# Attention outputs of six batches by seven products in a two-layer gated cross-attention kernel (one core)

## The chip, the cores and the metric

The kernel runs on one core of a Trainium2 chip. The metric is the device time of one launch in microseconds (us); the time of a version is the median of its runs. The engines are TensorE (PE; its weight loads are shown apart as PEld), VectorE (DVE), ScalarE (ACT), GpSimd (POOL) and SyncE (SP), which starts the DMAs. Each engine works through its own queue in order. Matrix products are written to PSUM, in banks of 512 float32 values for each of 128 partitions; an engine must read a bank out before it is written anew.

## The reference

Everything is float32. `x` is 8 batches of 512 tokens by 512 features; `ctx` is 8 batches of 120 keys by 512 features.

```python
x = x + tanh(g_xattn[0]) * L0_xattn(layernorm(x), ctx)         # 16 heads of 32, no mask
x = x + tanh(g_ffn[0])   * L0_ffn(layernorm(x))                # routed: 32 experts x 4 sets
x = x + tanh(g_xattn[1]) * L1_xattn(layernorm(x), ctx, mask)   # with biases
x = x + tanh(g_ffn[1])   * L1_ffn(layernorm(x))                # channel mix: gate, key, value

# an attention:
q, k, v = heads(y @ Wq.T), heads(ctx @ Wk.T), heads(ctx @ Wv.T)
out = softmax(q @ k.T / sqrt(32)) @ v          # for each head
return merge(out) @ Wo.T
```

The change touches the two attentions: the product with `Wo` above all, and the order of the work around it.

## The kernel before

**Tiles.** The 4096 tokens are 32 tiles of 128, four to a batch. `CrossAttention` is built twice (layer 0 and layer 1) and goes through three parts.

**Load and prologue.** The constructor loads, projects the keys (L342), and calls `prologue`: the values of the batches (`project_values`, L361, four products of 512 columns for a batch; it also has VectorE take the layer-norm sums of batch b+3), the transposes of the normalized tokens of batches 0 and 1 (`transpose_x`, L421, with the copy by ScalarE at L422, and `normalize` on ScalarE at L406, two buffers), the queries of batch 0, and the scores of tile 0. Here the order of every engine's queue is that of the program text (`manual_schedule(engines=every)`).

**Slots.** `run` goes through tiles t. A slot is: the scores of tile t+1 (L489, into the two double banks of `p_s`), products that stand ahead of the transposes, the transposes of the probabilities of tile t (L546, into the same double banks), more products, then `attend` (L581). In `run` only TensorE (and SP in layer 1) keeps the order of the program; the queues of VectorE, ScalarE and GpSimd are put in order by the planner when the program is compiled, from when it takes each instruction to be ready. An instruction that is ready and comes first in the program goes first.

**Softmax of a tile** (`scores`): VectorE reduces a maximum over each half (L514, L525); ScalarE takes eight exponentials of 120 columns with their sums (L517, which free one double bank); VectorE subtracts (L527, which frees the other), ScalarE takes one exponential of 960 columns (L528); VectorE sums (L533); GpSimd scales twice (L507).

**Seven products.** The queries of a batch (512 x 512 x 512) are done by `SevenProducts`: the two matrices are cut in quarters, and seven products of quarter sums take the place of eight. One product is `multiply`: four matmuls of 256 columns, which the profile shows as eight instructions (L149), since a float32 matmul is two. The sums of weights are taken once, those of tokens for each batch (L107).

**Outputs.** `output` takes four matmuls of 512 columns for a tile (L598, eight instructions), and VectorE adds the bank, times the gate, to `x` (L607). `run` splits them: two or three of the four ahead of the transposes, the rest behind.

**Banks.** `p_mm` has four single banks for everything else: query products, outputs, transposed tokens, `attend`.

**Late transposes.** `transpose_probs_late` (L567) takes four single banks of `p_mm` instead of the two of `p_s`, so that it need not wait for the exponentials of the next tile; VectorE copies one of the four (L569), ScalarE three (L571). Before the change only `tail` uses it, for the last five tiles.

**Beside attention.** `after` calls `RoutedFfn.in_slot` in layer 0 (layer-norm, a DMA of the tile to DRAM, transposes L722, routing products L731, three tiles behind) and `ChannelMix.in_slot` in layer 1.

Of the kernel before, what the change touches and what calls it, by code (L numbers as in the profile page):

```python
# [17 lines left out]
P = 128  # L18
# [53 lines left out]
class SevenProducts:  # L72
# [24 lines left out]
    @staticmethod  # L97
    def right_steps(w, t1, t2, t3, t4, engine):

        b11, b12, b21, b22 = [quarter(w, c, h) for c in (0, 1) for h in (0, 1)]

        def step(*args):
            return lambda: engine.tensor_tensor(*args)  # L107

        return [
            step(t3, b22, b12, ALU.subtract),  # L110
            step(t1, b12, b11, ALU.subtract),
            step(t2, b22, t1, ALU.subtract),
            step(t4, t2, b21, ALU.subtract),
        ]
# [91 lines left out]

class CrossAttention:
# [7 lines left out]
    def __init__(  # L215
        self, cm, tc, es, ins, gate, mask=None, biases=None, loads=(), then=None, vpool=None
    ):
        self.cm, self.nc, self.tc, self.gate, self.then = cm, cm.nc, tc, gate, then
        self.masked, self.biased = mask is not None, biases is not None
        nc = cm.nc  # L220

        def pool(name, bufs, **kw):
            pool = tc.tile_pool(name=name, bufs=bufs, reuse_waits="tile", **kw)
            return es.enter_context(pool)

        self.pool = pool("at_w", 1)
        vpool = vpool or self.pool
        self.norm = pool("at_n", 2)
        self.soft = pool("at_soft", 2)
        self.p_mm = pool("at_mm", 4, space=PSUM)  # L230
        self.p_s = pool("at_s", 2, space=PSUM)
        self.wq = self.pool.tile([P, NC, D], FP, name="wq")
        self.wo = self.pool.tile([P, NC, D], FP, name="wo")
        self.kT = self.pool.tile([P, NC, B * LK], FP, name="kT")
        self.v = [vpool.tile([P, 2, D], FP, name=f"v{q}") for q in range(B // 2)]
        self.xn, self.xnT, self.qT, self.probs, self.aT = {}, {}, {}, {}, {}
        self.ops = {}

        def right(name):
            return tc.tile_pool(name=name, bufs=1, side="right", reuse_waits="tile")  # L240

        with right("at_v") as self.vp:
            with right("at_k") as self.kp:
                self.load(ins, list(loads), mask, biases)
                if self.biased:
                    self.scale_biases()
                self.project_keys()
                if self.biased:
                    nc.gpsimd.tensor_scalar(self.gbo, self.gbo, self.gate, None, ALU.mult)
                for t in range(2):  # L250
                    self.normalize(t)
                if self.masked:
                    self.make_mask()
                self.sum_query_weights()
                for b in (1, 2):
                    self.stats_of_batch(b)
            self.work = pool("at_work", 2)
            self.prologue()

    def load(self, ins, loads, mask, biases):  # L260
# [4 lines left out]

        wv = self.soft.tile([P, NC * D], FP, name="wv", tag="pr")
        self.wv = wv.rearrange("p (c f) -> p c f", c=NC)
# [108 lines left out]
    def prologue(self):  # L376

        for b in range(3):
            self.project_values(b)
        for t in range(2 * TB):  # L380
            self.transpose_x(t)
            self.normalize(t + 2)
            if t < TB - 1:
                self.project_values(t + 3)
            elif t < 2 * TB - 1:
                self.queries(0, t + 1 - TB)
        rest = self.scores(0)
        for b in range(B - 2, B):
            self.project_values(b)
        rest()  # L390

# [21 lines left out]
    def transpose_x(self, t):  # L413
        nc = self.nc
        b, i = divmod(t, TB)
        if i == 0:
            self.xnT[b] = self.work.tile([P, NC, S + 1], FP, name="xnT")
# [4 lines left out]
        nc.scalar.copy(self.xnT[b][:, :, i * P : (i + 1) * P], ps)  # L422
        if i == TB - 1:
            self.start_queries(b)
# [9 lines left out]

    def start_queries(self, b):

        xnT = self.xnT[b][:, :, :S]
        own = self.work.tile([P, 2, 256], FP, name="xns", bufs=1)
        sums = [quarter(xnT, 0, 1), quarter(xnT, 0, 0), own, quarter(xnT, 1, 0)]
        engine = self.nc.gpsimd if b > 1 else self.nc.vector  # L440
# [4 lines left out]
        self.xn7 = SevenProducts.right(xnT, *sums)  # L445

    def queries(self, b, f):

        if f == 0:
            self.qT[b] = self.work.tile([P, NC, S], FP, name="qT")  # L450
            self.q7 = SevenProducts(
                self.nc,
                lambda: self.p_mm.tile([P, 2, 256], FP, name="qps", tag="mm"),
                self.wq7,
                self.xn7,
                {(i, j): quarter(self.qT[b], i, j) for i in (0, 1) for j in (0, 1)},
                lambda: quarter(self.xnT[b], 0, 1),
                bias=(self.bqk[:, 0, 0:2], self.bmore) if self.biased else None,
            )
        self.q7.next(2 if f < TB - 1 else 1)  # L460
        if f == 0:
            for step in self.later_sums:
                step()
# [110 lines left out]
    def attend(self, t):  # L574
# [13 lines left out]
        self.aT[t] = self.work.tile([P, NC, P], FP, name="aT")  # L588
        nc.scalar.copy(self.aT[t], aps)  # L589

    def output(self, t, chunks):

        nc, x = self.nc, self.cm.x
        if 0 in chunks:
            self.ops[t] = self.p_mm.tile([P, D], FP, name="ops", tag="mm")
        ops = self.ops[t]
        for c in chunks:
            nc.tensor.matmul(  # L598
                ops,
                self.aT[t][:, c, :],  # L600
                self.wo[:, c, :],
                start=(c == 0),
                stop=(c == NC - 1),
            )
        if NC - 1 in chunks:
            del self.ops[t], self.aT[t]
            nc.vector.scalar_tensor_tensor(  # L607
                x[:, t, :], ops, self.gate, x[:, t, :], ALU.mult, ALU.add
            )
# [6 lines left out]

    def run(self):

        for t in range(-1, NT - TB - 1):
            if t >= 0:  # L620
                if t + 10 < NT:
                    self.normalize(t + 10)
                self.scores(t + 1)()
            self.queries(*divmod(t + TB + 1, TB))
            self.after(t, 0)


            short = t % TB == TB - 2
            ahead = 3 if short else 2
            if t > 0:  # L630
                self.output(t - 1, range(ahead))
            x_ahead = short and not self.masked
            if x_ahead and t + 9 < NT:
                self.transpose_x(t + 9)
            if t >= 0:
                self.transpose_probs(t)
            if t > 0:
                self.output(t - 1, range(ahead, NC))
            if t + 9 < NT and not x_ahead:
                self.transpose_x(t + 9)  # L640
            self.after(t, 1)
            if t >= 0:
                self.attend(t)
            self.after(t, 2)

    def tail(self):

        for t in range(NT - TB - 1, NT + 1):
# [3 lines left out]
            self.output(t - 1, range(NC))  # L652
# [9 lines left out]
class RoutedFfn:  # L662
# [12 lines left out]
    def __init__(self, cm, tc, es, gate, ins):  # L675
# [5 lines left out]
        self.xT, self.perm = {}, {}  # L681

# [72 lines left out]

    def in_slot(self, s, attention, stage):

        last = NT - TB - 1
        if stage == 2 and 0 <= s - 1:
            self.route_stats(s - 1)  # L760
        if (stage == 2 and (0 <= s - 1 < last - 1 or s == NT)) or (stage == 3 and s > last):
            self.route_norm(s - 1 if stage == 2 else s - 2)
        if stage != (0 if s == NT else 1):
            return
        pool = attention.p_mm
        if s == -1:
            self.start()
        if 0 <= s - 4:
            self.route_logits(s - 4, pool.tile([P, D], FP, name="rlps", tag="mm"))
        if 0 <= s - 3:  # L770
            self.route_x(s - 3, pool.tile([P, D], FP, name="rxps", tag="mm"))
        b = (s - 9) // TB
        if (s - 9) % TB == 0 and 0 <= b < B - 2:
            self.route_back(b, pool.tile([P, D], FP, name="pps", tag="mm"))
# [256 lines left out]
class ChannelMix:  # L1031
# [57 lines left out]
    def in_slot(self, s, attention, stage):  # L1089
# [3 lines left out]
        if stage == 2 and 0 <= s - 2 < NT - 2 * TB:  # L1093
            attention.stats(s - 2)
# [17 lines left out]
        i = s - (NT - 10)  # L1112
        if 0 <= i - 1 < TB:
            self.transpose(i - 1)
        if 0 <= i < TB:
            xn = self.at.norm.tile([P, D], FP, name="xn")
            self.normalize(i, xn)
# [35 lines left out]
    def transpose(self, t):  # L1153
# [3 lines left out]
        if i == 0:  # L1157
            self.yT[b] = self.at.work.tile([P, NC, S + 1], FP, name="yT", tag="xnT")
# [30 lines left out]
    def sum_steps(self, b, m, engine=None):  # L1189
        engine = engine or self.nc.vector  # L1190
        at, mix = self.at, self.mix[b, m]
        if m == 1:
            sums = at.work.tile([P, 4 * 2 * 256 + NC], FP, name="xks", tag="xnT")
# [274 lines left out]
```

## Time and profile before

| | |
|---|---|
| median of 3 runs (lowest, highest) | 1437.04 us (1433.01 to 1438.22) |
| the profiled execution | 1433.48 us, of which the span from the first to the last instruction is 1431.7 us |
| ACT, POOL busy | 772.3 us (54%), 643.9 us (45%) |
| mean granted TensorE clock | 0.998 |

| window of the span, us | what runs | TensorE busy, us |
|---|---|---|
| 10 to 42 | keys, layer 0 | 30.70 |
| 42 to 116 | values, prologue, first slots, layer 0 | 71.24 |
| 166 to 215 | slots, layer 0 | 49.00 of 49.00 |
| 410 to 470 | tail, layer 0 | 59.30 |
| 470 to 690 | routed FFN | 204.66 of 220.00 |
| 722 to 800 | values, prologue, first slots, layer 1 | 75.37 |
| 900 to 1065 | slots, layer 1 | 165.00 of 165.00 |
| 1065 to 1135 | tail, layer 1 | 65.85 |
| 1135 to 1432 | channel mix | 287.72 of 297.00 |

Four slots (one batch) take 49.5 us in layer 0 (the same output group starts at 213.93 and 263.47 in the chain that ended last) and 44.4 us in layer 1 (840.78 and 885.14). The page's row for an engine is its busy time; a row for a group of instructions has the busy time of the group and the mean duration of one. Matmuls overlap in the pipe, so the spacing of their starts is what one costs, not its duration.

### The profile page before, as it was taken

To read this page: it belongs to the slowest core of one execution; us is meant where nothing else is said; L and a number is where in the kernel's file an instruction comes from. 1 tells how busy PE (TensorE), PEld (TensorE's weight loads), DVE (VectorE), ACT (ScalarE), POOL (GpSimd) and SP (SyncE) were. 2 spreads that over 40 slices of the span, in tenths; PEclk is the share of its full clock that TensorE was granted. 3 is DMA by queue.
4 is the path that set the end of the run, shared out by engine and by line. 5 is a ranking of instruction groups with operands and counts; after the bars stand their busy time and mean duration, and the time that the engine had idled before them with its cause. 6 is when DMAs were issued, how large, how long until landed. Compare 5 with 4: busy or idle time off the path is not lost.

```text
span 1431.7 us, 32559 instructions
## 1 busy us (share of the span) xinstructions
PE 1384.2 (97%) x13728; PEld 1068.2 (75%) x13728; DVE 1025.1 (72%) x1457; ACT 772.3 (54%) x1874; POOL 643.9 (45%) x576
## 2 busy tenths in 40 slices
PE   7999999999999998999999999999998999999997
PEld 3577777777776787888557777777776788888886
DVE  2666777777777676777576777777778588887786
ACT  1256666666666445444225665666656555445543
POOL 1425545545443001555375665665646333343331
PEclk9999999999999999999999999999999999999999
DMA  9200000000001347433301000000000000000001
GB/s 300 107 9 24 24 23 23 24 23 16 24 31 46 127 135 231 120 105 87 117 0 60 2 1 2 1 2 2 2 30 2 1 30 30 31 30 30 30 16 45
DMA packets 44886, 69.46 MB, mean 49 GB/s; under 512 B 2891, under 2 KB 20811, under 8 KB 44739
## 3 DMA queue, kind: packets, MB, share of 16 engines
q1 hardware_dynamic: 44451, 67.37, 14.6%
q8 instruction: 108, 1.77, 0.5%
q14 instruction: 39, 0.32, 0.1%
q10 hardware_dynamic: 288, 0.00, 0.0%
HBM read 50.59 MB, written 16.78 MB: 47 GB/s over the span
## 4 chain that ended last, share of the span: by engine, by line
PE 72%; DVE 14%; ACT 6%; POOL 4%; issue 3%; DMA 1%; POOLq 0%; DVEq 0%; ACTq 0%
PE ops L598 15%; PE qps L149 13%; PE tps L546 6%; PE cps L149 5%; PE aps L581 5%; PE s L489 4%; PE kps L342 4%; PE rps L992 3%; PE vps L361 3%; PE rlps L731 2%; PE l1ps L907 2%; PE ops L1013 2%; PE xnps L421 2%; PE l2ps L959 2%; PE gps L880 2%
## 5 line engine op out<-in xcount | busy, mean ns | idle before, releaser
L507 POOL TENSOR_TENSOR pr<-pr,rs 128x960 f32<-128x960 f32 x128 | 228.8, 1790 | 251.9 <-DVE rs L506 233.5
L598 PE MATMUL ops<-wo,aT 128*128 128x512 f32 x512 | 239.6, 594 | 0.7 <-ACT aT L589 0.7
L517 ACT ACTIVATE pr<-s,nmx 128x120 f32<-128x120 f32 x512 | 177.4, 372 | 114.0 <-DVE nmx L514 107.8
L598 PEld LDWEIGHTS ops<-wo,aT 128*128 128x128 f32 x512 | 92.1, 190 | 71.9 <-issue 67.0
L1005 POOL TENSOR_TENSOR r<-r,b 128x1024 f32<-128x1024 f32 x31 | 73.5, 2377 | 142.6 <-ACT r L1004 142.6
L149 PE MATMUL qps<-xnT,wq 128*128 128x256 f32 x512 | 119.6, 381 | 0.0
L546 PEld LDWEIGHTS tps<-ident,pr 128*120 128x120 f32 x864 | 96.8, 138 | 29.5 <-issue 26.2
L525 DVE TENSOR_REDUCE mx<-s 128x8 f32<-128x960 f32 x64 | 74.0, 1156 | 56.9 <-PE s L489 56.9
L517 ACT ACTIVATION_READ_ACCUMULATOR pr<-s,nmx 128x1 f32 x512 | 111.3, 217 | 0.0
L546 PE MATMUL tps<-ident,pr 128*120 128x128 f32 x864 | 104.7, 273 | 2.5 <-ACT pr L517 1.4
L149 PEld LDWEIGHTS qps<-xnT,wq 128*128 128x128 f32 x512 | 95.7, 189 | 15.2 <-issue 1.0
L533 DVE TENSOR_REDUCE sm<-pr 128x8 f32<-128x960 f32 x64 | 73.6, 1150 | 22.1 <-ACT pr L528 22.0
L49 DVE BATCH_NORM_STATS2 bnst<-x 128x6 f32<-128x512 f32 x128 | 86.8, 678 | 1.3
L422 ACT COPY xnT<-xnps 128x512 f32<-128x512 f32 x64 | 38.1, 595 | 82.0 <-PE xnps L421 82.0
L514 DVE TENSOR_REDUCE nmx<-s 128x8 f32<-128x960 f32 x64 | 73.5, 1149 | 6.8 <-PE s L489 6.8
L581 PE MATMUL aps<-prT,v 120*32 120x128 f32 x2048 | 73.3, 278 | 4.5 <-ACT prT L571 2.6
L527 DVE TENSOR_TENSOR pr<-s,mx 128x960 f32<-128x960 f32 x64 | 73.6, 1150 | 0.9
L1258 POOL TENSOR_TENSOR x<-x,cv 128x512 f32<-128x512 f32 x28 | 41.4, 1479 | 70.8 <-DVE cv L1255 70.8
L556 ACT COPY prT<-tps 120x1024 f32<-120x1024 f32 x54 | 55.0, 1019 | 32.9 <-PE tps L546 32.9
L489 PE MATMUL s<-kT,qT 32*128 32x120 f32 x2048 | 71.4, 276 | 0.0
L489 PEld LDWEIGHTS s<-kT,qT 32*128 32x128 f32 x2048 | 66.1, 187 | 6.5 <-issue 6.3
L581 PEld LDWEIGHTS aps<-prT,v 120*32 120x32 f32 x2048 | 53.8, 110 | 18.8 <-issue 8.3
(189 smaller groups left out, 3101.1 us busy)
## 6 DMA issues: line engine op xcount, KB each, us to landing
w<-in_w_dram SPq DMA_DIRECT2D x32, 512.0 KB, 4.8
x<-in_x_dram SPq DMA_DIRECT2D x8, 1024.0 KB, 15.4
aside<-x SPq DMA_DIRECT2D x32, 256.0 KB, 2.0
x<-aside SPq DMA_DIRECT2D x8, 1024.0 KB, 9.8
out_dram<-x SPq DMA_DIRECT2D x14, 512.0 KB, 2.8
ctx<-in_ctx_dram SPq DMA_DIRECT2D x4, 960.0 KB, 11.8
wk<-in_wk_dram SPq DMA_DIRECT2D x3, 1024.0 KB, 11.1
wv<-in_wv_dram SPq DMA_DIRECT2D x3, 1024.0 KB, 5.5
```

What stands on the lines that cost most here:

```text
L49: cm.nc.vector.bn_stats(st, cm.x[:, t, :])
L149: self.nc.tensor.matmul(ps[:, m, :], self.a[a][:, k, m * P : (m + 1) * P], self.b[b][:, k, :], start=(k == 0), stop=(k == 1),)
L489: nc.tensor.matmul(s[j // 2][:, j % 2, hc * LK : (hc + 1) * LK], self.qT[b][r : r + 32, hc, toks], self.kT[r : r + 32, hc, keys], start=no ...
L507: nc.gpsimd.tensor_tensor(pr[:, js, :, :], pr[:, js, :, :], rs[:, js, :, :].to_broadcast([P, 2, NC, LK]), ALU.mult,)
L514: nc.vector.tensor_reduce(nmx, sv[1], AX.X, ALU.max, negate=True)
L517: nc.scalar.activation(pr[:, 2 + j, hc, :], sv[1][:, j, hc, :], AF.Exp, bias=nmx[:, j, hc, :], accum_out=sm[:, 2 + j, hc : hc + 1],)
L525: nc.vector.tensor_reduce(mx, sv[0], AX.X, ALU.max)
L527: nc.vector.tensor_tensor(pv, sv[0], mx.to_broadcast([P, 2, NC, LK]), ALU.subtract)
L533: nc.vector.tensor_reduce(sm[:, :2, :], pv, AX.X, ALU.add)
L546: nc.tensor.transpose(ps[:, jj, hc * P : (hc + 1) * P], pr[:, 2 * u + jj, hc, :], self.cm.ident,)
L581: nc.tensor.matmul(aps[32 * j : 32 * j + 32, hc, :], self.v[b // 2][:LK, b % 2, h * HD : (h + 1) * HD], prT[:, j, hc, :], start=True, stop ...
L598: nc.tensor.matmul(ops, self.aT[t][:, c, :], self.wo[:, c, :], start=(c == 0), stop=(c == NC - 1),)
```

## The change

In `run`, the outputs of batches 0 to 5 are no longer made tile by tile. `SevenAdded`, a new kind of `SevenProducts`, makes them for a whole batch and adds each product from PSUM to the places in `x`, times the gate. The tokens of `attend` are kept for a batch in one buffer `aT`. The sums of tokens (`left_steps`) are taken on VectorE after the last `attend` of the batch, the sums of `Wo` once on GpSimd. `SevenAdded` and the query sums borrow quarters of the coming batch's `qT` as room. The outputs of the tiles of batches 6 and 7 are still made singly.

`slots` lists what stands ahead of the transposes and behind them in each slot. A slot whose tile is the last of a batch (t = 3, 7, ..., 23) uses `transpose_probs_late`, with one product and two token transposes ahead of it; the other three slots of a batch have three products ahead and one behind. `xnT` becomes a single buffer. In the prologue only the values of batches 0 to 4 are made; those of 5 to 7 move into slots 0 and 1. Routing and statistics follow in later slots.

```diff
+class SevenAdded(SevenProducts):
+    def __init__(self, nc, psum, a, b, c, t, gate, order):
+        super().__init__(nc, psum, a, b, c, None, order=order)
+        self.t, self.gate = t, gate
+    def add(self, c, ps):
+        self.nc.vector.scalar_tensor_tensor(c, ps, self.gate, c, ALU.mult, ALU.add)
+    def add_sum(self, *places):
+        for c in places:
+            self.nc.gpsimd.tensor_tensor(c, c, self.t, ALU.add)
+    def p1(self):
+        ps = self.multiply("A11", "B11")
+        self.nc.scalar.activation(self.t, ps, AF.Copy, scale=self.gate)
+        self.add_sum(self.c[0, 0])
+    def p2(self):
+        self.add(self.c[0, 0], self.multiply("A12", "B21"))
+    def p5(self):
+        ps = self.multiply("S1", "T1")
+        self.add(self.c[0, 1], ps)
+        self.add(self.c[1, 1], ps)
+    def p6(self):
+        self.add(self.t, self.multiply("S2", "T2"))
+        self.add_sum(self.c[0, 1])
+    def p7(self):
+        self.add(self.t, self.multiply("S3", "T3"))
+        self.add_sum(self.c[1, 0], self.c[1, 1])
+    def p3(self):
+        self.add(self.c[0, 1], self.multiply("S4", "B22"))
+    def p4(self):
+        self.add(self.c[1, 0], self.multiply("A22", "T4"))
...
     def prologue(self):
-        for b in range(3):
+        for b in range(2):
             self.project_values(b)
-        for t in range(2 * TB):
+        for t in range(TB):
             self.transpose_x(t)
             self.normalize(t + 2)
-            if t < TB - 1:
-                self.project_values(t + 3)
-            elif t < 2 * TB - 1:
-                self.queries(0, t + 1 - TB)
-        rest = self.scores(0)
-        for b in range(B - 2, B):
-            self.project_values(b)
+            if t == 1:
+                self.project_values(2)
+        self.start_queries(0)
+        self.queries(6)
+        self.project_values(3)
+        self.queries(1)
+        for t in range(TB, 2 * TB):
+            self.transpose_x(t)
+            if t + 2 < 2 * TB:
+                self.normalize(t + 2)
+            if t == TB:
+                rest = self.scores(0)
+        self.start_queries(1)
         rest()
+        self.project_values(4)
...
+    def start_outputs(self, b):
+        nc, aT = self.nc, self.aT
+        x = self.cm.x[:, b * TB : (b + 1) * TB, :]
+        c = self.quarters_of_queries(b + 2)
+        sums = [quarter(aT, 0, 1), c[0, 0], c[1, 1], c[0, 1]]
+        self.output_sums = SevenProducts.left_steps(aT, *sums, nc.vector)
+        self.o7 = SevenAdded(
+            nc, self.bank, SevenProducts.left(aT, *sums), self.wo7,
+            {(i, j): quarter(x, i, j) for i in (0, 1) for j in (0, 1)}, c[1, 0], self.gate,
+            "1256734",
+        )
...
+    def slots(self):
+        def tokens(t):
+            def step():
+                self.transpose_x(t)
+                if t % TB < 2:
+                    self.normalize(t + 2)
+            return step
...
+        yield [queries(2), values(5)], [queries(1)]
+        yield [queries(2), values(6)], [values(7)]
+        yield [queries(2), self.end_of_values], []
+        for b in range(B - 2):
+            t = TB * (b + 2)
+            yield [tokens(t), outputs(1), tokens(t + 1)], [outputs(1), tokens(t + 2)]
+            yield [tokens(t + 3), outputs(3)], [outputs(1)]
+            late = [[single(TB * b + TB + i)] for i in (0, 1)] if b == B - 3 else [[], []]
+            yield [outputs(1), queries(2)] + late[0], [queries(1)]
+            yield [queries(3)] + late[1], [queries(1)]
...
     def run(self):
...
+        for t, (ahead, behind) in zip(range(NT - TB - 1), self.slots()):
+            b, i = divmod(t, TB)
+            if i in (1, 2) and b + 2 < B:
+                self.normalize(TB * (b + 2) + i - 1)
+            self.scores(t + 1)()
+            if i == 3:
+                self.start_outputs(b)
             self.after(t, 0)
+            for piece in ahead:
+                piece()
+            (self.transpose_probs_late if i == 3 else self.transpose_probs)(t)
+            for piece in behind:
+                piece()
+            if t == TB - 2:
+                self.after(-1, 1)
             self.after(t, 1)
+            self.attend(t)
+            if i == 3:
+                for step in self.output_sums:
+                    step()
+            elif i == 0 and b > 0:
+                self.start_queries(b + 1)
             self.after(t, 2)
...
+    @staticmethod
+    def tiles_ended(s):
+        if s < 24:
+            return [s - 4] if s >= 4 else []
+        return {24: [20, 21], 25: [22, 23, 24]}.get(s, [s - 1])
...
+        if stage == (0 if s == NT else 1) or (stage == 0 and s in (last - 2, last - 1)):
+            t = self.t
+            if 0 <= t - 1:
+                self.route_logits(t - 1, bank("rlps"))
+            if 0 <= t:
+                self.route_x(t, bank("rxps"))
+            self.t += 1
```

`left_steps`, which was there before, takes the sums in this order: S3 = A11 - A21, S1 = A21 + A22 (written over A21), S2 = S1 - A11, S4 = A12 - S2.

## The prediction

> **What bounds the kernel.** I read the page's engine rows first, then the windows by stage, then the timelines of single slots.
>
> ```profile
> PE 1384.2 (97%) x13728; PEld 1068.2 (75%) x13728; DVE 1025.1 (72%) x1457; ACT 772.3 (54%) x1874; POOL 643.9 (45%) x576
> ```
>
> TensorE is busy for 97% of the span. The windows (us from the span's start, length, then busy time of PE, PEld, DVE, ACT, POOL) say where it is not.
>
> ```profile
> 166.00:215.00 49.00, 49.00 (x476) 37.87 (x475) 34.88 (x57) 32.61 (x94) 25.31 (x26) 1.00 0.06 23
> 900.00:1065.00 165.00, 165.00 (x1636) 121.01 (x1635) 122.02 (x171) 100.02 (x318) 94.41 (x77) 1.00 0.02 8
> ```
>
> In the slots it never rests: less TensorE work is worth its whole time there, and each wait that the change brings in costs its whole time too. So the question is how near the waits are. The timeline of TensorE in an early slot shows it.
>
> ```profile
> 91.37 1.17 PE L489 MATMUL s<-kT,qT 32*128 32x120 f32 x32
> 92.47 1.99 PE L149 MATMUL qps<-xnT,wqs 128*128 128x256 f32 x8
> 94.30 1.89 PE L149 MATMUL qps<-xnT,wq 128*128 128x256 f32 x8
> 96.74 1.06 PE L546 MATMUL tps<-ident,pr 128*120 128x128 f32 x8 [0.55 <-DVE pr L527]
> 98.47 1.09 PE L546 MATMUL tps<-ident,pr 128*120 128x128 f32 x8 [0.68 <-ACT pr L517]
> ```
>
> With only two products (3.7 us) between scores and transposes, TensorE waits 0.55 us for VectorE's subtraction and 0.68 us for ScalarE's exponentials. With 4.4 us (927.52 to 931.93, a slot of layer 1) it doesn't. The softmax chain after the scores is as long as the work put in front of it. How a late slot behaves, the tail of layer 0 tells, TensorE first, then ScalarE:
>
> ```profile
> 428.66 3.70 PE L598 MATMUL ops<-wo,aT 128*128 128x512 f32 x8
> 432.20 1.91 PE L567 MATMUL tps<-ident,pr 128*120 128x128 f32 x16
> 433.94 1.06 PE L731 MATMUL rlps<-rxT,wc 128*128 128x128 f32 x8
> 434.98 0.66 PE L722 MATMUL rxps<-ident,x 128*128 128x128 f32 x4
> 435.56 1.46 PE L581 MATMUL aps<-prT,v 120*32 120x128 f32 x32
> ```
>
> ```profile
> 432.70 1.04 ACT L528 ACTIVATE pr<-pr 128x960 f32<-128x960 f32 x1
> 433.60 0.85 ACT L714 ACTIVATE x<-x,nmr,rstd 128x512 f32<-128x512 f32 x1
> 434.31 1.59 ACT L571 COPY prT<-tps 120x512 f32<-120x512 f32 x3
> ```
>
> The three copies of late transposes go after the exponentials in ScalarE's queue and end at 435.90, 7.24 us after the scores (428.66); `attend` starts at 435.56 and stretches to 1.46 us instead of 1.08, waiting for them. The late form needs no double bank, but it needs ScalarE.
>
> **What goes.** In the chain, a long run of products costs
>
> ```profile
> 1372.00 46.64 PE cps L149 x216
> ```
>
> 0.216 us per instruction, 1.73 us for a product of eight. Four output instructions start 1.72 us apart (226.47 to the transposes at 228.19), so a tile is 3.44 and a batch 13.76 us; seven products are 12.09. Gain 1.67 us for a batch, **20.0 us** for twelve.
>
> One rule speaks against this. The Trainium skill ("TensorE: Matmul & The Clock Gate", section "The mechanism") says that a weight load overlaps with a running matmul only when it is for another group of rows. All these loads are 128x128, 190 ns in the group rows of L149 and L598, and a batch now has 56 instead of 32. With every load exposed: 56 x (0.190 + 0.216) - 32 x (0.190 + 0.43) = +2.9 us a batch, a loss of 35 us. The row of 216 decides: at 0.216 us apart, the loads lie beneath the matmuls. I take 20.0.
>
> **What is added beside.** VectorE: four sums (L107, 0.69 us alone) and seven adds from PSUM for four (L607, 0.74): 2.8 + 2.2 = 5.0 us a batch, on 122.02/165 x 44.4 = 32.8 in layer 1, to 37.8. GpSimd: four adds of some 1.2 us (L107 there 1.15) on 25.4. Neither becomes the bound over a batch; TensorE's own time hides them, except where TensorE waits for one of them, below. Once a layer the sums of `Wo` (4.6 us) lie on GpSimd between t=2 and their first use in slot 4, behind two scalings of 1.79; hidden. The moved values are the same products, and the end's single outputs, routing steps and DMAs (the one large DMA queue takes 14.6% of the 16 engines) the same number.
>
> **The slot of the last tile of a batch (t=3, 7, ..., 23): the large cost.** Zero is the end of the scores. TensorE ahead: tokens 0.44, product 1.84, tokens 0.44; late transposes 1.75; product 1.73; tokens 0.53: `attend` could start at 6.7 in layer 1, at 8.15 in layer 0 (routing, 0.90 and 0.53). ScalarE in layer 1, from the slot at 937.40: exponentials start at 2.43 (939.83), since VectorE has two maxima first, and run to 5.14; L528 to 6.0. Product 1 ends at 2.3 and is ready to be read at about 2.5, just too late to come before them. Behind them in program order stand its read-out (0.5), the copy of the second tokens (0.5), a `normalize` (0.75), then the three copies (1.55): 9.35, `attend` at 9.5. **Wait 2.8 us in layer 1.** Another order of the same work moves it little, as ScalarE has no rest in it. If the planner puts L528 and the `normalize` behind the copies: 1.1; with a route's L714 in front: up to 3.4. Banks say the same: product 1, the second tokens and two late transposes hold all four single banks until ScalarE comes to them at 6.0; the bank that VectorE empties goes to another transpose. The product behind the transposes starts at about 7.2 instead of 4.5: 2.7 us, which holds in layer 0 too, where routing would have hidden half of the wait for copies. I take 2.8 and 2.4: 6 x 2.8 + 6 x 2.4 = **+31.2 us** (ends 12 and 40).
>
> **The slot after it.** Product 5 needs S1, and S1 overwrites what S3 reads, so two sums stand after the copy of `aT`. That copy ends 0.82 us after the scores begin (947.73, 947.98, 0.57 long); two sums at 0.73 and 0.61 apart (80.05, 80.78, 81.39) and a release: 2.25. Scores and tokens take 1.2 + 0.44. Wait 0.6, twelve times: **+7.2 us**; it is 0 if the copy comes earlier, 2.5 if the sums meet GpSimd and take 1.7 each, as the longest L107 does. The maxima stand behind these sums, but 5.6 us of products lie ahead of the transposes and take that up. What stands behind product 5 in TensorE's queue is everything.
>
> **Prologue.** The scores of tile 0 are now followed by only two free token transposes (0.88 us). The third needs `normalize(7)`, which the written order puts in ScalarE's queue behind all exponentials of tile 0. Before, 7.1 us of values stood there. From the end of the values of batch 3: TensorE 1.73 + 0.44 + 1.10 + 0.88 = 4.15; VectorE 0.69, four pairs of statistics at 0.86, an add 0.69, maximum 1.07: 5.9; ScalarE 2.72 + 0.9 + copy 0.5 + 0.82: 10.9; with releases 11.1. Wait 6.9 us a layer (5.5 if the statistics were out of the way). The token sums T3, T1, T2 in front of product 6 cost 2.0 where 1.1 was. Gone are the early waits, 2.5 and 1.5 us. Net 5.3 + 6.3 = **+11.6 us**.
>
> **End of layer 0.** In slot 25 the routing transposes of tile 20 come right after the scores, some 3 us behind that tile's last output product. An add (0.74), statistics and GpSimd's scales (0.9 + 1.2; beside them the DMA of 2.0 us) and L714 (0.82) are 3.7, with what stands in the queues some 5.5 (an estimate). **+2.5 us** (0 to 6). `xnT` as a single buffer I cost at nothing: its last reader is a slot away.
>
> **Sum** against the profiled execution: 1433.5 - 20.0 + 31.2 + 7.2 + 11.6 + 2.5 = **1466.0**. Its own time is 3.6 us below the median of the runs, within their spread.
>
> **Rivals.**
> - *ScalarE's queue is kinder* (chance 0.18). The planner lets read-outs and copies pass; the late slot waits 1.1 us: +13 for 31.2, 1448. For: ScalarE is only 54% busy. Against: in the slot at 937.40 a read-out of a product ready at 939.4 ran at 943.44, behind all exponentials.
> - *The products win* (0.15), the other side: no wait in the late slots, because the maxima come so late there that the copies pass before the exponentials; 0.3 us for the sums, 8 for the prologue: 1433.5 - 20.0 + 3.6 + 8 = 1425. It decides from where the late slot's wait is under 0.5 us. The slots' 100% of TensorE is for it, ScalarE's load of the short slot against: eight copies and read-outs (0.53 each) and two `normalize`s (0.8) round the exponentials (3.6) come to 9.4 us, and TensorE's work there to 8.8.
> - *VectorE chokes* (0.11): sums at 1.7 us instead of 0.7 delay product 5 by 2 more: +24, 1490. Exposed loads (1521) are in this case.
> - *As worked out* (0.56): 1452 to 1482.
>
> **Chances.** A measurement here tells about 0.5% (7 us) from no change. Faster: most of the second rival, 0.12. Same: its rest and a little of the first, 0.07. Slower 0.81. The range 1430 to 1485 leaves out the fast rival's greater part and the choking one's.
>
> **What would show it.** Right: `attend` (L581) of late slots waiting for ScalarE's copies (L571) or the product before it for a bank, 2 to 3 us twelve times; a wait of 5 to 7 us at token transposes (L421) in each prologue; L149 instructions still 0.22 us apart. Wrong: TensorE at 100% in the slots and four slots in 42.7 and 47.8 us; then the time falls. Four slots of some 46 and 51 us are what I expect.

## The result, and the profile after

The changed kernel takes **1562.35 us** (median of 4 runs, 1560.87 to 1564.12), beside 1436.32 (4 runs, 1433.01 to 1438.22) before: a ratio of 1.0881, with a 95% interval of 1.0857 to 1.0904. It is slower, as forecast, but by 126 us where the sum said 32; the time lies far outside the range of 1430 to 1485. The engine row of the page comes first.

```profile
PE 1413.8 (90%) x14016; PEld 1146.8 (73%) x14016; DVE 1079.6 (69%) x1541; ACT 782.3 (50%) x1910; POOL 714.4 (46%) x632
```

The profiled span grew from 1431.7 to 1562.3 us, by 130.6. TensorE's rest (span less busy time) grew from 47.5 to 148.5, by 101.0. The other 29.6 us are more *busy* time, although an eighth of the output work of twelve batches (20.0 us by the prediction) went away. So two things have to be explained: new waits, and matmuls that became slower. The waits of TensorE in the changed kernel (engine, tile and line, what ended the wait, us in total, times, longest) show the first:

```profile
PE tps L610 <- ACT pr L581: 24.1, 16, 3.7
PE tps L631 <- ACT qT L226: 23.6, 12, 2.0
PE aps L645 <- DVE prT L618: 12.4, 16, 1.6
PE qps L149 <- DVE aT L88: 10.7, 12, 1.6
...
PE aps L645 <- ACT prT L620: 7.8, 6, 2.4
PE tps L631 <- DVE prT L633: 6.1, 12, 0.5
```

L631 is the late transposes, L610 the ordinary ones (before, this row was `PE tps L546 <- ACT pr L517: 1.4, 2, 0.7`), L149 with `aT` the output product that needs a sum, L645 `attend`. The first and third rows, 36.5 us, belong to no step of the prediction. Three single waits follow further down: 4.8 us of the routing's transposes (L842) for L834, and 3.7 and 3.5 of the scores in the two prologues for L591. The windows by stage, with the columns of the table of before, show the second:

```profile
166.00:215.00 49.00, 42.69 (x450) 36.53 (x449) 33.01 (x51) 27.80 (x77) 22.66 (x21) 0.97 0.03 12
900.00:1065.00 165.00, 143.52 (x1442) 120.50 (x1442) 125.88 (x174) 90.89 (x289) 104.67 (x82) 0.98 0.01 1
```

TensorE falls from 100% to 87% in both. The column behind GpSimd's, the granted clock, was 1.00 in both windows and is 0.97 and 0.98. Over the whole span the mean clock went from 0.998 to 0.973. The clock record of the trace holds only full and half, so that is (1 - 0.973) x 2 x 1562.3 = 84 us at half clock instead of 6: up to 39 us lost. The prediction had no term for it. Some 10 us of added busy time (29.6 + 20.0 - 39) stay unexplained.

**The late slot** is the one that was foreseen. TensorE's timeline in layer 0 (start, length, ..., idle time before it and what ended it):

```profile
191.19 0.65 PE L631 MATMUL tps<-ident,pr 128*120 128x128 f32 x4 [1.96 <-ACT qT L226]
191.68 3.21 PE L149 MATMUL qps<-wo,aT 128*128 128x256 f32 x8
194.68 1.06 PE L473 MATMUL xnps<-ident,xn 128*128 128x128 f32 x4
```

And ScalarE's:

```profile
189.52 1.04 ACT L592 ACTIVATE pr<-pr 128x960 f32<-128x960 f32 x1
190.41 0.72 ACT L226 ACTIVATE qT<-qps,gates 128x512 f32<-128x512 f32 x1
```

The read-out of the first product stands behind all the exponentials; the fourth group of late transposes gets its bank at 191.19, when that read-out is done. The wait is 1.96 us, with 0.51 us for VectorE's copy 2.6 us ahead of it. But the product that follows is spread over 3.00 us (191.68 to 194.68); at full clock it takes 1.82 (371.29 to 373.11, the same place three batches later). The clock in windows of 1 us explains it:

```profile
192.00:193.00 1.00, 1.00 (x5) 0.79 (x4) 0.00 (x0) 1.00 (x3) 1.00 (x1) 0.63 0.00 0
193.00:194.00 1.00, 1.00 (x4) 0.81 (x3) 0.00 (x0) 0.77 (x2) 1.00 (x2) 0.50 0.00 0
194.00:195.00 1.00, 1.00 (x5) 0.70 (x4) 0.01 (x1) 0.00 (x0) 0.84 (x1) 0.50 0.00 0
195.00:196.00 1.00, 1.00 (x8) 1.00 (x7) 0.74 (x1) 0.17 (x1) 0.00 (x0) 0.66 0.00 0
```

The last column but two is the granted clock. What is missing from it adds up to (0.37 + 0.50 + 0.50 + 0.34) x 2 = 3.4 us at half clock, just behind the wait, while TensorE is busy again. That costs up to 1.7 us, so the wait of 1.96 us is nearly paid for a second time.

**The slot after it, layer 1**, is where the forecast failed. VectorE's timeline:

```profile
949.68 1.39 DVE L88 TENSOR_TENSOR qT<-aT 128x512 f32<-128x512 f32 x1 [1.48 <-ACT aT L652]
951.11 0.69 DVE L88 TENSOR_TENSOR aT<-aT 128x512 f32<-128x512 f32 x1
...
952.56 1.64 DVE L88 TENSOR_TENSOR qT<-aT,qT 128x512 f32<-128x512 f32 x1
954.13 1.15 DVE L589 TENSOR_REDUCE mx<-s 128x8 f32<-128x960 f32 x1
```

And TensorE's:

```profile
951.95 1.97 PE L149 MATMUL qps<-wos,aT 128*128 128x256 f32 x8 [1.36 <-DVE aT L88]
...
959.33 1.09 PE L610 MATMUL tps<-ident,pr 128*120 128x128 f32 x8 [0.72 <-ACT pr L581]
...
963.28 1.08 PE L645 MATMUL aps<-prT,v 120*32 120x128 f32 x32 [1.13 <-DVE prT L618]
```

Here L88 is the sums of tokens. The scores are there at 950.0, but their maximum starts at 954.13, behind all four sums. From 949.68 until its copy for `attend` ends at 963.2 VectorE rests for 0.7 us. TensorE first waits for a sum (1.36), then for exponentials that the late maxima delay (0.72), then for VectorE's copy (1.13): 3.2 us in one slot, each for VectorE or for what it delayed. From the first sum to the end of that copy VectorE is busy for 12.74 of 13.54 us (94%), and from there to the first sum of the next batch (at 1001.03) for 25.43 of 37.81 (67%).

**Slot 1 of each batch in layer 0** holds a wait that no view of before had. GpSimd's timeline, and below it ScalarE's:

```profile
212.89 1.28 POOL L222 TENSOR_TENSOR x<-x,qT 128x512 f32<-128x512 f32 x1
...
215.41 1.27 POOL L107 TENSOR_TENSOR xnT<-xnT 128x512 f32<-128x512 f32 x1
216.78 0.22 POOL L58 TENSOR_SCALAR ve<-mv 128x1 f32<-128x1 f32 x1
```

```profile
218.03 0.81 ACT L834 ACTIVATE x<-x,nmr,rstd 128x512 f32<-128x512 f32 x1 [5.43 <-POOL nmr L61]
...
220.08 0.34 ACT L581 ACTIVATE pr<-s,nmx 128x120 f32<-128x120 f32 x1
```

The new output adds (L222) and query sums (L107) stand ahead of the tiny scales (L58 to L61) on GpSimd. The routing's normalization (L834) waits 5.43 us for those scales at the head of ScalarE's queue, and the exponentials, which have nothing to do with it, stand behind. TensorE waits 3.66 us for them (at 222.96) and its next product then takes 2.57 us at the lower clock.

### The profile page after: what moved, and what is told of

It reads as the page before. It is cut to its first block, busy times and chain, and to the rows that moved or that the text cites. A ratio compares the mean times of both kernels' runs of the same rounds, so it can differ in the third digit from the quotient of the medians.

```text
span 1562.3 us, 33377 instructions
## 1 busy us (share of the span) xinstructions
PE 1413.8 (90%) x14016; PEld 1146.8 (73%) x14016; DVE 1079.6 (69%) x1541; ACT 782.3 (50%) x1910; POOL 714.4 (46%) x632
## 4 chain that ended last, share of the span: by engine, by line
PE 48%; DVE 25%; ACT 14%; POOL 5%; issue 5%; DMA 1%; ACTq 0%; POOLq 0%; DVEq 0%; SPq 0%
PE qps L149 10%; ACT pr L581 6%; PE cps L149 4%; PE kps L390 4%; PE ops L663 3%; PE aps L645 3%; PE vps L409 3%; PE rps L1128 3%; PE s L553 3%; DVE mx L589 3%; DVE nmx L578 2%; DVE qT L88 2%; PE tps L610 2%; PE l1ps L1043 2%; PE ops L1149 2%
## 5 line engine op out<-in xcount | busy, mean ns | idle before, releaser
L149 PE MATMUL qps<-xnT,wq 128*128 128x256 f32 x512 | 121.0, 384 | 0.0
L222 POOL TENSOR_TENSOR x<-x,qT 128x512 f32<-128x512 f32 x48 | 61.3, 1278 | 108.2 <-DVE qT L218 108.2
L610 PE MATMUL tps<-ident,pr 128*120 128x128 f32 x672 | 87.1, 280 | 25.6 <-ACT pr L581 24.1
L149 PEld LDWEIGHTS qps<-xnT,wq 128*128 128x128 f32 x512 | 96.0, 191 | 14.9
L610 PEld LDWEIGHTS tps<-ident,pr 128*120 128x120 f32 x672 | 76.8, 140 | 39.8 <-ACT pr L581 29.1
L645 PE MATMUL aps<-prT,v 120*32 120x128 f32 x2048 | 74.8, 278 | 22.9 <-DVE prT L618 12.4
L645 PEld LDWEIGHTS aps<-prT,v 120*32 120x32 f32 x2048 | 54.3, 110 | 43.2 <-DVE prT L618 20.5
L631 PE MATMUL tps<-ident,pr 128*120 128x128 f32 x352 | 49.6, 285 | 31.1 <-ACT qT L226 23.6
L553 PEld LDWEIGHTS s<-kT,qT 32*128 32x128 f32 x2048 | 67.8, 190 | 11.8 <-issue 11.6
L591 DVE TENSOR_TENSOR pr<-s,mx 128x960 f32<-128x960 f32 x64 | 73.5, 1149 | 0.8
L218 DVE SCALAR_TENSOR_TENSOR x<-qps,gates,x 128x512 f32<-128x512 f32 x60 | 43.6, 743 | 40.1 <-PE qps L149 37.2
```

Source lines behind the costliest of these rows:

```text
L149: self.nc.tensor.matmul(ps[:, m, :], self.a[a][:, k, m * P : (m + 1) * P], self.b[b][:, k, :], start=(k == 0), stop=(k == 1),)
L553: nc.tensor.matmul(s[j // 2][:, j % 2, hc * LK : (hc + 1) * LK], self.qT[b][r : r + 32, hc, toks], self.kT[r : r + 32, hc, keys], start=no ...
L591: nc.vector.tensor_tensor(pv, sv[0], mx.to_broadcast([P, 2, NC, LK]), ALU.subtract)
L610: nc.tensor.transpose(ps[:, jj, hc * P : (hc + 1) * P], pr[:, 2 * u + jj, hc, :], self.cm.ident,)
L645: nc.tensor.matmul(aps[32 * j : 32 * j + 32, hc, :], self.v[b // 2][:LK, b % 2, h * HD : (h + 1) * HD], prT[:, j, hc, :], start=True, stop ...
```

## The experiments

The theory after the result: 1562 is the foreseen late slot, plus exponentials blocked behind the routing's normalization, plus the half clock that follows waits, plus VectorE and GpSimd as bounds of single slots. The rival: the three-ahead order of the slots is bad as such, so that single repairs only move the waits. All times are medians; ratios are against the kernel before, run beside it.

**e1: no late slot.** Every slot uses ordinary transposes; the slot of the last tile has two output products ahead.

```diff
-            yield [tokens(t), outputs(1), tokens(t + 1)], [outputs(1), tokens(t + 2)]
+            yield [tokens(t), outputs(1), tokens(t + 1), outputs(1)], [tokens(t + 2)]
-            (self.transpose_probs_late if i == 3 else self.transpose_probs)(t)
+            self.transpose_probs(t)
```

> The slot of a batch's last tile takes the ordinary transposes, with both of its output products ahead of them. Theory (ScalarE's queue and the four single banks hold up the late transposes, 2.5 us, and the clock then runs at half for one piece of 3.41 us, some 1.4 us more): the waits of L631 vanish, attend waits up to 1 us more, so 2.7 to 3.7 us less for each of twelve batches: 1562 - 32 to 1562 - 45, that is 1517 to 1530 us. Rival (VectorE is full, and a wait taken away comes back at the next place that it feeds): above 1550 us, with longer waits of attend for VectorE's copy.

1545.8 us, ratio 1.0761 (1.0737 to 1.0785): only 16.5 less. The 29.7 us of waits at L631 (23.6 and 6.1 above) are gone, but `attend` now waits 18.5 us for ScalarE's copies (7.8 before the edit) and the product with S1 14.3 (10.7). The theory's size was too large by half: part of a removed wait came back one instruction later, and the mean clock stayed low (0.975).

**e2: the routing's normalization on GpSimd**, so that its wait no longer blocks ScalarE (tiles 0 to 23).

```diff
-        nc.scalar.activation(
-            x, x, AF.Identity, bias=self.cm.nmr[:, t, :], scale=self.cm.rstd[:, t, :]
-        )
+        rstd, nmr = self.cm.rstd[:, t, :], self.cm.nmr[:, t, :]
+        if t < 24:
+            nc.gpsimd.tensor_scalar(x, x, rstd, nmr, ALU.mult, ALU.add)
+        else:
+            nc.scalar.activation(x, x, AF.Identity, bias=nmr, scale=rstd)
```

> The routing's normalization of tiles 0 to 23 moves from ScalarE to GpSimd, in layer 0 alone. Theory (in the second slot of a batch the exponentials stand behind that normalization in ScalarE's queue, which waits for GpSimd's scales): the wait of 3.7 us before the second half of the transposes vanishes, with the 0.6 at attend and part of the slow clock, 4 to 5 us for each of six batches: 1533 to 1540 us; layer 1 unchanged. Rival (GpSimd is late because it is full): the wait moves to the transposes of the routing or to the scaled probabilities, above 1550 us.

1540.55 us, 1.0730 (1.0701 to 1.0759), 21.8 less, although GpSimd got more work; just outside the range of the theory. The transposes' waits for the exponentials fall from 24.1 to 6.3 us:

```profile
PE tps L610 <- ACT pr L581: 6.3, 13, 0.7
```

So this queue, and not the number of products ahead, held them up in layer 0. The new waits for query sums on GpSimd (L107), 8.8 us, are the price.

**e3: the prologue's first scores after all token transposes.**

```diff
-            if t == TB:
-                rest = self.scores(0)
+        rest = self.scores(0)
         self.start_queries(1)
```

> In the prologue the scores of tile 0 come after all token transposes. Theory: TensorE's wait of 3.7 + 0.4 us there vanishes in both layers, and a slow piece of 6.8 us (3.4 us of time) with it: 7 us a layer less, 1548 us. Rival (the early waits come back in slot 0, since the statistics still stand before the first maxima on VectorE): 1556 to 1562 us.

1559.74 us, 1.0859 (1.0825 to 1.0892), 2.6 less: as the rival said, and no more than the noise, since its interval and that of the changed kernel (1.0857 to 1.0904) overlap. The two waits at the scores (3.7 and 3.5) disappear, but 3.0 us of waits at token transposes and longer ones of `attend` take their place.

**e4: e1, e2 and e3 together.**

> The three edits together. Theory (three separate waits, each with its slow clock): the gains add up, 1562 - 74 = 1488 us, between 1478 and 1500, and less than 25 us at half clock is left. Rival (one full engine behind all): less than two thirds of the sum, above 1512 us.

1517.68 us, 1.0567 (1.0534 to 1.0600): 44.7 less, where the single ones sum to 41.0. They add up, but the expectation had counted on 74; by its terms the rival is met (less than two thirds of 74, above 1512), and 42 us at half clock are left where it had under 25. More than half of the loss is elsewhere; the largest waits left are S1 (14.2 us) and `attend` for copies (13.2 on ScalarE, 12.2 on VectorE).

**e5: useless work in the wait.** Four matmuls of 256 columns into a scores' bank stand between the third and the fourth late transposes of the twelve late slots: 12 x 1.73 = 20.8 us of work that nobody needs.

```diff
+        fill = t < NT - TB - 1
...
+            if fill and j == 1:
+                idle = self.p_s.tile([P, 2, 512], FP, name="idle", tag="s")
+                for _ in range(4):
+                    nc.tensor.matmul(
+                        idle[:, 0, :256], self.cm.ident, self.wo[:, 0, :256],
+                        start=True, stop=True,
+                    )
```

> The changed kernel with four useless products of 256 columns (1.73 us) in each late slot, between the third and the fourth late transposes, where TensorE waits 1.97 us for ScalarE; they write to a double bank that VectorE has emptied by then, and nothing reads them. Theory (the wait itself makes the clock fall to half, which costs some 1.4 us more each time): TensorE comes out of the wait at the same moment but at full clock; the time at half clock falls from 85 us to 45 or less, and the kernel gets 10 to 20 us faster for 21 us of added work: 1542 to 1552 us. Rival (the slow clock has another cause, or added work is added time): half clock as before, 1562 us or up to 20 us more.

1549.26 us, 1.0792 (1.0774 to 1.0810): **13.1 us faster with more work**. TensorE's timeline (the late transposes are L639 in this run's kernel):

```profile
187.44 0.66 PE L639 MATMUL tps<-ident,pr 128*120 128x128 f32 x4 [0.24 <-ACT qT L226]
187.93 1.98 PE L149 MATMUL qps<-wo,aT 128*128 128x256 f32 x8
```

The fourth group of transposes waits 0.24 us instead of 1.96, since the useless work fills the rest. But the product behind it takes 1.81 us (187.93 to 189.74) instead of 3.00. The mean clock rises from 0.973 to 0.979, which is some 18 us less at half clock. That these waits drop the clock is shown. Of the 13.1 us, the clock can explain 9 (half of 18); most of the rest is `attend`'s waits for its two copies, 16.2 us instead of 20.2. The expectation of the total half-clock time (45 us or less) was missed, with 65: other waits still cause it.

**e6: a rearranged slot list.** e2 and e3, ordinary transposes everywhere with the last query product moved into the last tile's slot, S4 behind the next maxima, and the end's doubled routing one slot later.

```diff
-            yield [tokens(t), outputs(1), tokens(t + 1)], [outputs(1), tokens(t + 2)]
+            rest = [queries(1)] if b else []
+            yield [tokens(t), *rest, outputs(1), tokens(t + 1)], [outputs(1), tokens(t + 2)]
...
-                for step in self.output_sums:
+                for step in self.output_sums[:3]:
```

> The three repairs and three more: the last query product of a batch moves into the slot of the batch's last tile (three products there, ordinary transposes), S4 is taken behind the next maxima, and the doubled routing steps come one slot later. Theory (waits of single places, in reach of the order): most of the 36 us of waits at attend, and at S1 their clock share, go: 1470 to 1490 us, with less than 25 us at half clock. Rival (VectorE over its whole queue is late by what the sums and adds put on it): 1500 us or more, attend waiting for VectorE's copy in three of four slots.

1499.93 us, 1.0449 (1.0434 to 1.0465), at the rival's edge. This order is worth 62 us of the 126; others weren't tried. TensorE's waits that are left (L609 is the transposes, L644 `attend` in this run's kernel):

```profile
PE qps L149 <- DVE aT L88: 15.5, 12, 2.3
PE tps L609 <- ACT pr L580: 14.7, 22, 0.9
PE aps L644 <- DVE prT L617: 13.2, 14, 2.8
```

**e7: the changed kernel without the four sums of tokens** (plain quarters are multiplied in their place). **e8: the kernel before with 448 of the 512 output columns** for the first six batches, which takes an eighth of this output work away, as the seven products do, and adds nothing.

```diff
 e7
-            nc, self.bank, SevenProducts.left(aT, *sums), self.wo7,
+            nc, self.bank, SevenProducts.left(aT, *[quarter(aT, 0, 0)] * 3, quarter(aT, 1, 0)), self.wo7,
...
-                for step in self.output_sums:
-                    step()
+                pass
 e8
+        n = 448 if t < NT - 2 * TB else D
...
-                self.wo[:, c, :],
+                self.wo[:, c, :n],
```

> The changed kernel without the four sums of tokens for the outputs; products 5, 6, 7 and 3 take plain quarters of aT in their place. Theory (the wait for S1 is one among several): its 10.7 us go, with what the delayed maxima cost in that slot, 20 to 28 us less: 1534 to 1542 us; the late slots' waits stay at 2.5 us. Rival (VectorE full): more than 40 us less, and the waits of attend for VectorE's copy vanish everywhere.

> The kernel before, with an eighth of the output columns of batches 0 to 5 left out (448 of 512 for each matmul), which takes from TensorE what the seven products take and adds nothing. Theory (TensorE's time in the slots is worth its whole): 20 us less, 1417 us, between 1412 and 1422. Rival (the softmax chain holds the slots as much as TensorE does, so that the gain was never to be had): less than 8 us, waits for the exponentials before the transposes in place of it.

e7: 1527.70 us, 1.0645 (1.0629 to 1.0661), 34.6 less, between the two expectations. VectorE's busy time fell by 40.0 us (1079.6 to 1039.6), so most of the time that the sums took on VectorE was paid by the kernel. Of TensorE's waits, that for S1 is gone, and those for the exponentials and for VectorE's copy shrink from 24.1 and 12.4 us to

```profile
PE tps L610 <- ACT pr L581: 15.0, 7, 3.6
...
PE aps L645 <- DVE prT L618: 3.4, 7, 1.6
```

so the sums did delay the maxima and the copies. The late slots' waits stay (23.7 and 6.1 us). e8: 1422.28 us, 0.9914 (0.9889 to 0.9938): the whole benefit that the slots of before can take from the shorter work is 13.5 us, not 20.0, although TensorE is busy for 19.6 us less (1384.2 to 1364.6); the transposes' waits for the exponentials grow from 1.4 us to 4.8 (14 of them) and take part of the rest.

**e9, e10, e11: e6 without the sums, without GpSimd's adds, without both.** Again work is left out: e9 multiplies plain quarters, e10 doesn't spread the shared products over the outputs.

```diff
 e9
-                for step in self.output_sums[:3]:
-                    step()
+                pass
 e10
-        for c in places:
-            self.nc.gpsimd.tensor_tensor(c, c, self.t, ALU.add)
+        pass
```

> The arrangement of e6 (1499.9 us) without the four sums of output tokens on VectorE; plain quarters are multiplied in their place. Theory (what is left of the loss is mainly VectorE's and GpSimd's added work, which I had costed at nothing): 25 to 35 us less, 1465 to 1475, and the waits of the product that needs S1 (15.5 us) and of attend for VectorE's copy (13.2 us) nearly gone. Rival (what is left is the order of the slots, too little work between scores and transposes): under 12 us less, above 1488, and the transposes' waits for the exponentials (14.7 us) take over what is set free.

> The arrangement of e6 (1499.9 us) without the four adds of a batch on GpSimd that spread a shared product over the outputs. Theory (they stretch VectorE's sums from 0.69 to 1.6 us and stand ahead of the query sums in GpSimd's queue): 8 to 18 us less, 1482 to 1492, sums back at about 0.7 us, and the wait for the query sums (8.7 us) gone. Rival (GpSimd's adds lie beside everything): less than 4 us.

> The arrangement of e6 without the four sums and without the four adds. Theory (added work on VectorE and GpSimd is most of what is left): 1440 to 1460, half of the way or more back to the kernel before (1436) less the products' 13.5 us. Rival (the order of the slots is most of what is left): 1475 or more.

| kernel | us | ratio to before (95%) | less than e6 |
|---|---|---|---|
| e6 | 1499.93 | 1.0449 (1.0434 to 1.0465) | |
| e9 no sums | 1457.92 | 1.0160 (1.0139 to 1.0181) | 42.0 |
| e10 no adds | 1482.43 | 1.0331 (1.0309 to 1.0352) | 17.5 |
| e11 neither | 1449.89 | 1.0105 (1.0087 to 1.0124) | 50.0 |

The totals of e10 and e11 lie in the theory's ranges; e9's gain, 42.0 us, is larger than its 25 to 35. The waits of TensorE in e9, to set beside the three of e6 above:

```profile
PE tps L609 <- ACT pr L580: 11.5, 14, 0.9
...
PE aps L644 <- DVE prT L617: 6.2, 7, 2.9
```

VectorE's busy time is 46.6 us less (1091.4 to 1044.8), and the kernel's 42.0. The wait for S1 is gone and `attend`'s wait for VectorE is halved; most of the wait for the exponentials stays. In e10 the wait for the query sums (8.7 us in e6) is gone, as expected, but another expectation failed: without GpSimd's adds the sums are not short. VectorE in e10, then GpSimd:

```profile
974.01 1.64 DVE L88 TENSOR_TENSOR aT<-aT 128x512 f32<-128x512 f32 x1
```

```profile
973.36 1.74 POOL L463 TENSOR_TENSOR x<-x,gbo 128x512 f32<-128x512 f32 x1
```

Other work of GpSimd, which the kernel had all along, lies beside them instead; its 1.74 us here are 1.26 when VectorE doesn't sum (975.52).

No version of the changed kernel beat the kernel before. Even e11, which does none of the added sums and adds, is 1% slower than it.

## Why the prediction was wrong

- **The step that failed** is the one headed "What is added beside": "Neither becomes the bound over a batch; TensorE's own time hides them". It set 37.8 us of VectorE against a batch of 44.4, a mean over four slots, and expected batches of some 46 us in layer 1 and 51 in layer 0; they took 51.5 (943.42 to 994.91, the same late transposes) and 59.7 (191.19 to 250.91). The four sums all fall into one slot, ahead of the maxima that its transposes need. In the changed kernel the sums cost 34.6 us (e7); in the rearranged one they cost 42.0 and GpSimd's adds 17.5, 50.0 together (e9 to e11), where the sum had 7.2 for the S1 wait and nothing else. The sentence that 5.6 us of products would take up the late maxima was the same fault: the maximum started 4.1 us after the scores' end, and the copies for `attend` came later still.
- **A queue was left out.** Of the moved routing the prediction counted instructions and priced only the end of layer 0, as +2.5 us (its wait was 4.8). It said nothing of what stands behind L834 on ScalarE when GpSimd's scales come late. That is worth 21.8 us (e2).
- **The clock was left out.** About 78 us more at half clock, up to 39 lost; 13.1 us net came back when only the late slots' waits were filled (e5), 9 of them by the clock at most, with 20.8 us of useless work put in.
- **The late slot** was right in mechanism and in the size of its wait: 23.6 + 6.1 = 29.7 us measured for 31.2 predicted. It stands at a bank, which the prediction named as the other face of the late copies, though at the last transposes, which need the first product's, and not at the product behind them. Its worth isn't 29.7: removing it gave 16.5 (e1).
- **The wait for S1** measured 10.7 us for 7.2. The alternative "the sums meet GpSimd and take 1.7 each" was written down as an end of the range and is what happened in part: 1.39 and 0.69 us in the slot shown, 1.64 and 1.72 in another (1051.80 and 1053.47).
- **The products' gain** was mis-sized: 13.5 us for 20.0 (e8). The 0.22 us between instructions was right; that all of TensorE's saved time would come out at the end was not.
- **The prologue** was mis-sized and misplaced. The large wait is not at token transposes but at the scores, 3.7 and 3.5 us. Moving the scores returned 2.6 us, within the noise (e3); the rest of the 11.6 wasn't tested.
- **The rival "VectorE chokes"** had the right engine and the wrong size, 1490: it delayed only product 5, not the maxima behind the sums.

What stays open: the sums' cost is shown, but that it comes from their falling into one slot is read from the trace (VectorE is busy for 94% of the time there and for 67% in the rest of the batch); no run spread them over the slots. And e11 is 27.6 us above e8, which saves as much of the output work. Half clock (0.993 beside 0.999) is up to 8 us of it. Its list of waits has 11.6 us of transposes waiting for exponentials and 5.8 of `attend` for VectorE's copy, which fits the changed slots, but no run took these apart. The terms also overlap: the single effects of e2, e5 and e7 can't simply be added.

## What to carry to other kernels

Check an engine's added work in the one slot where it falls and in front of the work that it will stand before, not only over the mean of a loop: VectorE was busy for 72% of the span before, and 46.6 us of sums on it cost the kernel 42.0. For every moved instruction that waits, list what stands behind it in its queue, though it has nothing to do with it. Where TensorE is near 100%, price a new wait with the clock that may drop behind it, and add up the waits that lie close together.

## What the runs showed of the hardware

**Short waits drop the clock.** The twelve late slots have the same two waits, 0.51 and 1.96 us. In nine of them the product behind took 2.66 to 3.10 us, in three 1.82. The slow stretches in the trace's clock record last 3.41 us or twice that (the last is cut by the record's end), and all begin on one grid of 3.41 us. For waits of this length, the place on the grid decides. Divide the span from 22 us on into the windows of this grid, and take those at full clock, 426 in the changed kernel: 12 had 2.0 us or more without a matmul, and the clock fell to half behind each; 404 had less than 1.84 us, and it fell behind none; of the 10 between, it fell behind 7. In the nine slow late slots one window held 1.85 to 2.48 us without a matmul; in the three others the grid splits them, and no window held more than 1.81. In all 13 traces it fell behind 92 of 92 windows with 2.0 us or more, behind none of 5212 with less than 1.4, and behind 42 of the 150 between. With the wait filled (e5), the product took 1.81 to 1.83 us in all twelve late slots. The Trainium skill ("TensorE: Matmul & The Clock Gate", section "HAM oscillation — how this bites in real kernels") gives as the rule that no gap of TensorE should exceed some 3.4 us. The length of the slow stretch agrees with that figure; the threshold does not, since a gap of 1.96 us was enough here. By that rule the twelve late slots would have lost nothing; by the trace nine of them lost about 1.1 us each in the product behind (2.88 on average less 1.82), and what else ran at half clock.

**VectorE's sums and GpSimd block each other.** A sum of two SBUF operands takes 0.69 us alone and 1.64 beside GpSimd, and GpSimd is slowed in turn (e10). The Trainium skill ("SBUF — State Buffer", section "SBUF: two separate sides") says that such a VectorE instruction and GpSimd exclude each other for a whole instruction. The trace agrees. In the slot shown, the sum at 951.11, with GpSimd at rest, takes 0.69 us; the one at 952.56 takes 1.64 and ends at 954.20, 0.55 us behind this instruction of GpSimd:

```profile
951.99 1.66 POOL L465 TENSOR_TENSOR x<-x,gbo 128x512 f32<-128x512 f32 x1 [1.47 <-ACT xn L461]
```
